# Rows two to a partition, 2 KB runs and one residual tile per unit in a graph-convolution kernel

## The chip, the cores and the metric

The kernel runs on one core of a Trainium2 chip. The metric is the device time of one execution in microseconds (us). The kernel before takes 1714.94 us, the median of the four runs beside which the changed kernel was timed; the prediction was made from three runs with a median of 1718.39 us.

## The reference

```python
# x: (8, 4096, 256), adj: (4096, 4096) sparse, W: (256, 256), all f32
HW = einsum('bnf,fo->bno', x, W)
A_norm = relu((adj + adj.T) * 0.5)
D = sum(A_norm, axis=1);  d = where(D > 0, D ** -0.5, 0)
L = eye(N) - d[:, None] * A_norm * d[None, :]
out = layernorm(x + relu(einsum('nm,bmo->bno', L, HW)))    # over the 256 features
```

## The kernel before

**Part A** symmetrises `adj` tile by tile into DRAM, sums the degrees, and forms g, the rows of HW scaled by d. A *form* makes 128 rows of g for all eight batches. TensorE transposes x, ScalarE copies the transposes from PSUM, TensorE multiplies by W, and ScalarE copies the result out. For every form two symmetrised tiles are made in the first half of part A, and one later on.

```python
def form(m, known):                            # 32 of these
    xin = ...; nc.sync.dma_start(xin, x[:, m*P:(m+1)*P, :]...)     # 1 KB runs
    for b in range(0, B, 2):                   # 4 x 4 = 16 transposes
        pt = psum.tile(...)
        ... nc.tensor.transpose(pt[:, k, c, :], xin[:, b+k, ...], ident)
        nc.scalar.copy(xt[:, b:b+2], pt)
    for b in range(0, B, 2):                   # 4 x 8 matmuls (two passes each)
        ... nc.tensor.matmul(pg..., lhsT=xt[:, b+k, c, :], rhs=w_sb[:, c, :], ...)
        nc.scalar.mul(to, pg, r[:, m:m+1])     # or a copy, scaled later ("held")
    nc.scalar.dma_start(g_dram[m*P:(m+1)*P, :], g)                 # 8 KB runs
```

**Part B** makes the output in sixteen units of 256 rows, each of two blocks of 128. A unit needs only the columns in which its rows have an entry. Lists of these columns are sorted by *pattern* (which of the unit's four groups of 64 rows have an entry) and gathered by indirect DMA into a ring of 13 tiles. `CAPS` gives each unit its number of tiles per pattern. Tiles that are not full cost TensorE as much as full ones. Then for each block:

```python
def finish(i):
    y = evict(i, py.pop(i), ypool)             # ScalarE: PSUM -> SBUF with relu
    def rest():
        z = xr.pop(i)
        mv, rstd = moments(i, y, z, stat)      # VectorE: z += y, statistics
        def end():
            normalise(i, z, mv, rstd)          # VectorE, then store of 1 MB from SyncE
            if i + 3 < NB:
                xr[i+3] = residual(i+3, ypool) # load of 1 MB, issued from ScalarE
        after(6, end)                          # six matmul steps later
    after(1, rest)
...
xr = ypool.tile([P, B, F], F32, tag="xr", bufs=4)       # the residual buffers
...
after(2, lists, u)    # lists of later units: small matmuls into two PSUM banks of
                      # block 0's tag, then some 25 VectorE operations on them
```

VectorE runs in program order, so the list operations of a unit stand behind the residual add of that unit's block 0.

Of the kernel before, what the change touches and what calls it, by code (L numbers as in the profile page):

```python
# [18 lines left out]
KINDS = [1, 2, 3, 0, 6, 9, 5, 10, 12, 4, 8]  # L19

CAPS = [
    [5, 2, 4, 12, 1, 2, 3, 1, 1, 1, 1],
    [4, 3, 2, 6, 1, 1, 1, 1, 1, 3, 3],
    [4, 3, 1, 4, 1, 1, 1, 1, 1, 3, 3],
    [3, 3, 1, 3, 1, 1, 1, 1, 1, 3, 3],
    [4, 3, 1, 3, 1, 1, 1, 1, 0, 3, 3],
    [3, 3, 1, 2, 1, 1, 1, 1, 1, 3, 3],
    [3, 3, 0, 3, 1, 1, 1, 1, 0, 3, 3],
    [3, 3, 0, 2, 1, 1, 1, 1, 1, 3, 3],
    [3, 3, 0, 2, 1, 1, 1, 1, 1, 3, 3],  # L30
    [3, 3, 0, 4, 0, 0, 0, 1, 0, 3, 3],
    [3, 3, 1, 1, 1, 1, 1, 1, 1, 3, 3],
    [3, 3, 0, 4, 0, 0, 0, 0, 0, 3, 3],
    [3, 3, 0, 4, 0, 0, 0, 0, 0, 3, 3],
    [3, 3, 0, 4, 0, 0, 0, 0, 0, 3, 3],
    [3, 3, 1, 3, 0, 0, 0, 0, 0, 3, 3],
    [3, 3, 1, 3, 0, 0, 0, 0, 0, 3, 3],
# [3 lines left out]
def kernel(  # L41
# [6 lines left out]
):  # L48

# [26 lines left out]
    Q = 64  # L76
    QU = 4
    HOLD = 8
# [5 lines left out]
    mid = KINDS.index(0), KINDS.index(12)  # L84
# [12 lines left out]
    e = const.tile([P, NB], F32, name="e")  # L97
    r = const.tile([P, NB], F32, name="r")
# [45 lines left out]
    own = const.tile([P, QU, 2], F32, name="own")  # L144
    nc.vector.memset(own, 0.0)
    for s in range(QU):
        h = slice((s % 2) * Q, (s % 2 + 1) * Q)
        nc.vector.memset(own[h, s, s // 2 : s // 2 + 1], 1.0)
# [14 lines left out]
    def patterns(u):  # L163

        used = ipool.tile([P, QU, NB], F32, tag="used", name=f"used_{u}", bufs=1)
        nc.vector.tensor_scalar(
            used, part[:, :, u * QU : (u + 1) * QU].rearrange("p m s -> p s m"), 0.0, None, ALU.is_gt
        )
        diag = used[:, :, 2 * u : 2 * u + 2]
        nc.vector.tensor_tensor(diag, diag, own, ALU.max)  # L170
        two = ipool.tile([P, 2, NB], F32, tag="two", name=f"two_{u}", bufs=1)
        uv = used.rearrange("p (b h) m -> p b h m", b=2)
        nc.vector.scalar_tensor_tensor(two, uv[:, :, 1], 2.0, uv[:, :, 0], ALU.mult, ALU.add)
        pat = ipool.tile([P, NB], F32, tag="pat", name=f"pat_{u}")
        nc.vector.scalar_tensor_tensor(pat, two[:, 1], 4.0, two[:, 0], ALU.mult, ALU.add)
        kind = ipool.tile([P, NK, NB], BF16, tag="kind", name=f"kind_{u}")
        nc.vector.tensor_tensor(
            kind,
            pat.unsqueeze(1).to_broadcast([P, NK, NB]),
            kinds.unsqueeze(2).to_broadcast([P, NK, NB]),  # L180
            ALU.is_equal,
        )
        plan[u] = pat, kind
# [34 lines left out]
    def place_rest(u, tot, low):  # L218
# [3 lines left out]
        room = CAPS[u][mid[0]] * P  # L222
# [4 lines left out]
            pos, pos, float(first[u][mid[0]] * P + 1), fits, ALU.add, ALU.mult  # L227
# [47 lines left out]
    def index(u, pl):  # L275
# [9 lines left out]
        m0, m1 = first[u][mid[0]], first[u][mid[1]]  # L285
        for ts, n, k in ((slice(0, m0), NB, 2 * u), (slice(m0, m1), NU, u), (slice(m1, t), NB, 2 * u + 1)):
            nc.vector.tensor_scalar(
                ai[:, ts], low[:, ts], float(n), float(N * n + k), ALU.mult, ALU.add
            )
# [3 lines left out]
    with (  # L293
        tc.tile_pool(name="adj", bufs=4) as apool,
        tc.tile_pool(name="hold", bufs=HOLD) as hpool,
# [14 lines left out]
        def symmetrise(i, j, tij, tji):  # L310
            sym = spool.tile([P, A, S], F32, tag="sym", name=f"sym_{i}_{j}")
            for a in range(A):
# [6 lines left out]
            nc.scalar.activation(sym, sym, AF.Relu, scale=0.5)  # L319
            nc.vector.tensor_reduce(  # L320
                part[:, i * A : (i + 1) * A, j * S // Q : (j + 1) * S // Q],
                sym.rearrange("p a (c q) -> p a c q", q=Q),
# [10 lines left out]
        def degrees(i):  # L333
# [6 lines left out]
            nc.gpsimd.tensor_tensor(r[:, ms], e[:, ms], neg_half[:, :A], ALU.pow)  # L340
# [17 lines left out]
        def form(m, known):  # L358

            xin = xpool.tile([P, B, F], F32, tag="xin", name=f"xin_{m}")  # L360
            nc.sync.dma_start(xin, x[:, m * P : (m + 1) * P, :].rearrange("b p f -> p b f"))
            xt = xpool.tile([P, B, FC, P], F32, tag="xt", name=f"xt_{m}", bufs=1)
            for b in range(0, B, 2):
                pt = psum.tile([P, 2, FC, P], F32, tag="ps", name=f"xtr_{m}_{b}")
                for k in range(2):
                    for c in range(FC):
                        nc.tensor.transpose(pt[:, k, c, :], xin[:, b + k, c * P : (c + 1) * P], ident)  # L367
                nc.scalar.copy(xt[:, b : b + 2], pt)  # L368
            if known:
                g = xpool.tile([P, G], F32, tag="g", name=f"gt_{m}")  # L370
            else:
                g = hpool.tile([P, G], F32, tag="held", name=f"held_{m}")
            for b in range(0, B, 2):
                pg = psum.tile([P, 2 * FO], F32, tag="ps", name=f"pg_{m}_{b}")
                for k in range(2):
                    for c in range(FC):
                        nc.tensor.matmul(  # L377
                            pg[:, k * FO : (k + 1) * FO],
                            lhsT=xt[:, b + k, c, :],
                            rhs=w_sb[:, c, :],  # L380
                            start=(c == 0),
                            stop=(c == FC - 1),
                        )
                to = g[:, b * FO : (b + 2) * FO]
                if known:
                    nc.scalar.mul(to, pg, r[:, m : m + 1])  # L386
                else:
                    nc.scalar.copy(to, pg)
            if known:
                nc.scalar.dma_start(g_dram[m * P : (m + 1) * P, :], g)  # L390
            else:
                held[m] = g

        def release(m):
            g = held.pop(m)
            if m % 2:
                nc.vector.tensor_scalar(g, g, r[:, m : m + 1], None, ALU.mult)
            else:
                nc.scalar.mul(g, g, r[:, m : m + 1])
            nc.scalar.dma_start(g_dram[m * P : (m + 1) * P, :], g)  # L400
# [3 lines left out]
        known, early = [], list(range(NB - HOLD, NB))  # L404
        credit = 0.0
        for i in range(NS):
            diag = stat1.tile([P, A, P], F32, tag="diag", name=f"diag_{i}")
            for j in range(i, NS):
# [6 lines left out]
                while credit >= 1.0 and (known or early):  # L415
                    if known:
                        form(known.pop(0), True)
                    else:
                        form(early.pop(0), False)
                    credit -= 1.0  # L420
                credit = min(credit, 1.0)
            degrees(i)
            for m in range(i * A, (i + 1) * A):
                if m in held:
                    release(m)
            lower_diagonal(i, diag)
            known += range(i * A, min((i + 1) * A, NB - HOLD))
# [18 lines left out]
        for m in known:  # L446
            form(m, True)


    def residual(i, ypool):  # L450
        xr = ypool.tile([P, B, F], F32, tag="xr", name=f"xr_{i}", bufs=4)
        nc.scalar.dma_start(xr, x[:, i * P : (i + 1) * P, :].rearrange("b p f -> p b f"))
        return xr
# [25 lines left out]
    def normalise(i, z, mv, rstd):  # L479
# [10 lines left out]
        nc.sync.dma_start(out[:, i * P : (i + 1) * P, :].rearrange("b p f -> p b f"), z)  # L490
# [25 lines left out]
    with (  # L516
# [10 lines left out]
        def gather(n):  # L527
# [5 lines left out]
            both = len(targets(kind)) == 2  # L533
# [28 lines left out]
        xr = {0: residual(0, ypool)}  # L562
# [3 lines left out]
        def finish(i):  # L566
            y = evict(i, py.pop(i), ypool)

            def rest():
                z = xr.pop(i)  # L570
                mv, rstd = moments(i, y, z, stat)

                def end():
                    normalise(i, z, mv, rstd)
                    if i + 3 < NB:
                        xr[i + 3] = residual(i + 3, ypool)
# [25 lines left out]
        after(4, lambda: xr.update({i: residual(i, ypool) for i in (1, 2)}))  # L602
        for q, (u, step) in enumerate(steps):
            new = q == 0 or steps[q - 1][0] != u
            last = q + 1 == len(steps) or steps[q + 1][0] != u
            if new:
                if u + 2 < NU:
                    spread(u + 2)
                if u + 4 < NU:
                    patterns(u + 4)  # L610
                left = {}
# [21 lines left out]
            for c in range(G // S):  # L633
                for (b, rows, at, gt), new_rows in zip(work, fresh):
                    both = any(len(targets(k)) == 2 for k, t in step)
                    off = b * P if both else 0
                    nc.tensor.matmul(  # L637
                        py[2 * u + b][c][rows, :],
                        lhsT=at[:, off + rows.start : off + rows.stop],
# [29 lines left out]
    with tc.If(short > 0):  # L669
        with (  # L670
# [5 lines left out]
            for i in range(NB):  # L676
                lt = full.tile([P, NB, P], F32, tag="l", name=f"l_{i}", bufs=2)
                nc.sync.dma_start(
                    lt, a_dram[:N, i * P : (i + 1) * P].rearrange("(m p) q -> p m q", p=P)
                )  # L680
                py = [psum.tile([P, S], F32, tag="ps", name=f"pz_{i}_{c}") for c in range(G // S)]
                for m in range(NB):
                    gt = full.tile([P, G], F32, tag="g", name=f"gf_{i}_{m}", bufs=4)
                    nc.sync.dma_start(gt, g_dram[m * P : (m + 1) * P, :])
                    for c in range(G // S):
                        nc.tensor.matmul(
                            py[c],
                            lhsT=lt[:, m, :],
# [4 lines left out]
                y = evict(i, py, ypool)  # L693
                z = residual(i, ypool)
                mv, rstd = moments(i, y, z, stat)
                normalise(i, z, mv, rstd)
# [28 lines left out]
```

## Time and profile before

| | before |
|---|---|
| median | 1714.94 us (1702.32 to 1719.27) |
| part A: start to first gathered matmul | 568 us |
| part B: from there to the end | 1154 us |
| busy share of TensorE, VectorE, GpSimd, ScalarE | 88%, 47%, 48%, 21% |

### The profile page before, as it was taken

What the parts mean: (1) busy time and instruction counts of PE and PEld (TensorE: products, weight loads), DVE (VectorE), ACT (ScalarE), POOL (GpSimd) and SP (SyncE); (2) the same over time, 40 slices, a digit from 0 to 9 for tenths busy, and PEclk for the clock granted to TensorE, in tenths of its full rate; (3) what the DMA queues carried; (4) which work ended last, traced back from release to release, by engine and by line L of the source; (5) the groups of instructions that cost most, each with busy time, mean ns of one, the idle gap of its engine ahead of it and who ended that gap; (6) DMA issues with size and microseconds to landing.
All of it is one profiled execution on the core that took longest, in us unless ns stands there. A gap on an engine that the chain in (4) does not pass through costs nothing.

```text
span 1721.7 us, 18447 instructions
## 1 busy us (share of the span) xinstructions
PE 1508.8 (88%) x6504; PEld 799.3 (46%) x6504; DVE 802.5 (47%) x1832; ACT 357.8 (21%) x453; POOL 829.8 (48%) x1111
## 2 busy tenths in 40 slices
PE   6998787888893799999999999989979889898992
PEld 5887666777783244343433333333324333333330
DVE  4777698864553000241442624624633632641335
ACT  3655443555554000100010000000110110110011
POOL 3010000100012663575868777777777777676650
PEclk8999888899897899999999999999989999899996
DMA  9999989999998994688899999899899799799965
GB/s 333 383 377 371 401 331 394 341 405 378 361 363 336 400 397 154 238 336 291 326 405 343 359 378 365 313 402 356 331 398 369 256 404 364 284 342 369 346 260 182
DMA packets 230964, 591.34 MB, mean 343 GB/s; under 512 B 19781, under 2 KB 118389, under 8 KB 191173
## 3 DMA queue, kind: packets, MB, share of 16 engines
q0 software_dynamic: 58480, 321.34, 48.7%
q1 hardware_dynamic: 100352, 134.23, 22.3%
q10 hardware_dynamic: 72032, 134.51, 20.8%
q8 instruction: 54, 0.88, 0.2%
q14 instruction: 46, 0.38, 0.1%
HBM read 494.47 MB, written 136.34 MB: 366 GB/s over the span
## 4 chain that ended last, share of the span: by engine, by line
PE 32%; DMA 25%; issue 23%; DVE 14%; POOL 2%; ACT 2%; another core or an unknown queue 1%; ACTq 0%; DVEq 0%; POOLq 0%; SPq 0%
PE py L637 26%; DMA out_dram<-xr 12%; DMA xr<-in_x_dram 9%; PE pg L377 4%; DVE xr L482 3%; DVE stats L473 2%; DVE xr L468 2%; DVE sym L318 2%; DMA adj<-in_adj_dram 2%; DVE hot L244 1%; DMA xin<-in_x_dram 1%; ACT sym L319 1%; DVE part L320 1%; DMA a_dram<-sym 1%; PE xtr L367 1%
## 5 line engine op out<-in xcount | busy, mean ns | idle before, releaser
L637 PE MATMUL py<-g,ga 128*64 128x512 f32 (+1 forms) x3368 | 1046.8, 604 | 54.3 <-DMA g<-g_dram,gi 36.6
L637 PEld LDWEIGHTS py<-g,ga 128*64 128x64 f32 (+1 forms) x3368 | 395.9, 156 | 692.8 <-issue 661.6
L544 POOL DMA_INDIRECT g<-g_dram,gi x317 | 388.3, 1225 | 236.1 <-PE py L637 132.5
L535 POOL DMA_INDIRECT ga<-a_dram,ai x317 | 336.4, 1061 | 104.0 <-issue 97.3
L468 DVE TENSOR_TENSOR xr<-xr,y 128x2048 f32<-128x2048 f32 x32 | 73.3, 2289 | 634.7 <-ACT y L458 336.6
L458 ACT ACTIVATE y<-py,minus_r 128x512 f32<-128x512 f32 x128 | 80.5, 688 | 1068.2 <-PE py L637 455.0
L377 PE MATMUL pg<-w_sb,xt 128*128 128x256 f32 x1024 | 249.1, 400 | 30.4 <-ACT xt L368 30.0
L318 DVE TENSOR_TENSOR sym<-tr,adj 128x512 f32<-128x512 f32 x256 | 159.7, 682 | 159.2 <-PE tr L315 108.8
L377 PEld LDWEIGHTS pg<-w_sb,xt 128*128 128x128 f32 x1024 | 200.1, 200 | 71.8 <-ACT xt L368 42.9
L340 POOL TENSOR_TENSOR r<-e,neg_half 128x4 f32<-128x4 f32 x8 | 8.3, 1042 | 445.0 <-DVE e L339 389.8
L315 PE MATMUL tr<-ident,adj 128*128 128x128 f32 x1024 | 132.1, 288 | 46.2 <-DMA adj<-in_adj_dram 25.0
L319 ACT ACTIVATE sym<-sym 128x2048 f32<-128x2048 f32 x64 | 122.3, 1912 | 138.0 <-DVE sym L318 111.2
L315 PEld LDWEIGHTS tr<-ident,adj 128*128 128x128 f32 x1024 | 122.3, 149 | 56.0 <-issue 25.1
L320 DVE TENSOR_REDUCE part<-sym 128x32 f32<-128x2048 f32 x64 | 144.5, 2277 | 6.1 <-ACT sym L319 5.9
L482 DVE TENSOR_SCALAR xr<-xr,mv,rstd 128x256 f32<-128x256 f32 x256 | 87.0, 411 | 48.3 <-POOL rstd L480 48.3
L473 DVE BATCH_NORM_STATS2 stats<-xr 128x6 f32<-128x256 f32 x256 | 87.2, 411 | 0.7
L386 ACT ACTIVATE gt<-pg,r 128x512 f32<-128x512 f32 x96 | 66.1, 690 | 79.8 <-PE pg L377 79.8
L480 POOL TENSOR_TENSOR rstd<-rstd,neg_half 128x8 f32<-128x8 f32 x32 | 54.9, 1715 | 44.0 <-DVE rstd L476 43.4
L367 PE MATMUL xtr<-ident,xin 128*128 128x128 f32 x512 | 69.6, 290 | 5.0 <-DVE sym L318 4.8
L368 ACT COPY xt<-xtr 128x512 f32<-128x512 f32 x128 | 68.8, 582 | 14.6 <-PE xtr L367 10.7
L244 DVE TENSOR_TENSOR hot<-iota_q,at 128x4096 bf16<-128x4096 f32 x16 | 70.6, 4416 | 0.0
L367 PEld LDWEIGHTS xtr<-ident,xin 128*128 128x128 f32 x512 | 62.2, 150 | 9.1 <-DVE sym L318 8.3
(93 smaller groups left out, 378.4 us busy)
## 6 DMA issues: line engine op xcount, KB each, us to landing
adj<-in_adj_dram SPq DMA_DIRECT2D x64, 1024.0 KB
a_dram<-sym ACTq DMA_DIRECT2D x64, 1024.0 KB
xin<-in_x_dram SPq DMA_DIRECT2D x32, 1024.0 KB
xr<-in_x_dram ACTq DMA_DIRECT2D x32, 1024.0 KB
out_dram<-xr SPq DMA_DIRECT2D x32, 1024.0 KB
g_dram<-gt ACTq DMA_DIRECT2D x24, 1024.0 KB
g_dram<-held ACTq DMA_DIRECT2D x8, 1024.0 KB
ga<-a_dram,ai POOLq DMA_INDIRECT x317
```

What stands on the lines that cost most here:

```text
L315: nc.tensor.transpose(pt[:, c * P : (c + 1) * P], tji[:, c, a * P : (a + 1) * P], ident)
L318: nc.vector.tensor_add(sym[:, a, :], pt, tij[:, a, :])
L319: nc.scalar.activation(sym, sym, AF.Relu, scale=0.5)
L320: nc.vector.tensor_reduce(part[:, i * A : (i + 1) * A, j * S // Q : (j + 1) * S // Q], sym.rearrange("p a (c q) -> p a c q", q=Q), AX.X, A ...
L367: nc.tensor.transpose(pt[:, k, c, :], xin[:, b + k, c * P : (c + 1) * P], ident)
L377: nc.tensor.matmul(pg[:, k * FO : (k + 1) * FO], lhsT=xt[:, b + k, c, :], rhs=w_sb[:, c, :], start=(c == 0), stop=(c == FC - 1),)
L468: nc.vector.tensor_add(z, z, y)
L473: nc.vector.bn_stats(stats[:, b, :], z[:, b, :])
L482: nc.vector.tensor_scalar(z[:, b, :], z[:, b, :], mv[:, b, 0:1], rstd[:, b : b + 1], ALU.subtract, ALU.mult,)
L535: nc.gpsimd.indirect_dma_start(out=at if both else at[:, :P], out_offset=None, in_=a_pairs if both else a_rows, in_offset=bass.IndirectOff ...
L544: nc.gpsimd.indirect_dma_start(out=gt, out_offset=None, in_=g_dram, in_offset=bass.IndirectOffsetOnAxis(ap=gi[:, t : t + 1], axis=0), boun ...
L637: nc.tensor.matmul(py[2 * u + b][c][rows, :], lhsT=at[:, off + rows.start : off + rows.stop], rhs=gt[:, c * S : (c + 1) * S], start=new_ro ...
```

## The change

The intent is fewer and longer packets. A unit's 256 rows are laid two on each partition, so x, residual and result move in runs of 2 KB. A unit's two blocks become its even and its odd rows. One residual tile of 2 MB serves a unit, with two such buffers in place of four of 1 MB. The patterns are now of even and odd rows, so `KINDS` and `CAPS` change. In unit 0 the dense tiles go from 12 to 15. Forms are cut by rows and batches: one loads 256 rows of four batches and makes its even and odd half one after the other.

```diff
@@ form
-        def form(m, known):
-            nc.sync.dma_start(xin, x[:, m * P : (m + 1) * P, :].rearrange("b p f -> p b f"))
-            for b in range(0, B, 2):        # 16 transposes, four copies
-            for b in range(0, B, 2):        # 32 matmuls
-                nc.scalar.dma_start(g_dram[m * P : (m + 1) * P, :], g)
+        def form(u, b0, known):
+            nc.sync.dma_start(xin..., x[b0 : b0 + BH, u*2*P : (u+1)*2*P, :].rearrange("b (p k) f -> p b (k f)", k=2))
+            for k in range(2):
+                for b in range(0, BH, 2):   # 8 transposes, two copies
+                for b in range(0, BH, 2):   # 16 matmuls
+                put(u, b0, k, g)            # 512 KB, 4 KB runs
@@ degrees
-            nc.gpsimd.tensor_tensor(r[:, ms], e[:, ms], neg_half[:, :A], ALU.pow)
+            # four small matmuls by `perm` bring the degrees to the new order, then
+            nc.gpsimd.tensor_tensor(r[:, ms], own_e..., neg_half[:, :A], ALU.pow)
@@ part B
-        xr = ypool.tile([P, B, F], F32, tag="xr", name=f"xr_{i}", bufs=4)
-        nc.scalar.dma_start(xr, x[:, i * P : (i + 1) * P, :].rearrange("b p f -> p b f"))
+        z = ypool.tile([P, B, 2, F], F32, tag="z", name=f"z_{u}", bufs=2)
+        nc.scalar.dma_start(z.rearrange("p b k f -> p b (k f)"), rows_of(x, u))
@@
-                    normalise(i, z, mv, rstd)       # stores its block
-                    if i + 3 < NB:
-                        xr[i + 3] = residual(i + 3, ypool)
+                    normalise(i, z, mv, rstd)
+                    if b == 1:
+                        store(u, zs.pop(u))
@@ at the start of unit u
+                if u + 1 < NU:
+                    after(3, lambda v=u + 1: zs.update({v: residual(v, ypool)}))
@@ matmul
-                        lhsT=at[:, off + rows.start : off + rows.stop],
+                        lhsT=at[:, 2 * lo + b : 2 * (lo + rows.stop - rows.start) : 2],
```

(Comments stand for the lines that are left out; `CAPS`, `KINDS` and a fallback path are not shown.)

## The prediction

> **What bounds the kernel now.** I read the page's slices first, then a table of stretches, the chain that ended last, the timeline around one wait, and the DMA packets. The kernel has two parts: to 568 us it makes the symmetric matrix and the scaled features g (part A); then it multiplies sixteen units of 256 output rows with gathered tiles (part B). Columns of the stretches: start and end, length, busy time of PE, PEld, DVE, ACT, POOL, granted clock, DMA share, GB/s.
>
> ```profile
> 0.00:540.00 540.00, 443.35 (x2638) 387.09 (x2638) 367.29 (x536) 273.60 (x324) 48.14 (x441) 0.92 0.99 367
> ...
> 568.00:640.00 72.00, 71.82 (x170) 29.13 (x171) 0.00 (x0) 0.00 (x0) 47.91 (x50) 0.98 1.02 407
> 640.00:745.00 105.00, 105.00 (x349) 40.82 (x348) 24.43 (x72) 5.50 (x8) 49.73 (x42) 1.00 0.59 205
> 745.00:900.00 155.00, 153.47 (x562) 59.68 (x562) 49.70 (x153) 10.37 (x16) 104.07 (x92) 1.00 0.93 349
> ...
> 1100.00:1300.00 200.00, 185.35 (x756) 70.01 (x754) 99.96 (x284) 14.54 (x24) 153.30 (x127) 0.96 0.94 358
> 1300.00:1500.00 200.00, 178.40 (x654) 69.30 (x653) 91.58 (x279) 14.97 (x24) 145.01 (x118) 0.93 0.90 336
> ```
>
> Part A is DMA bound outright (0.99). Unit 0 (568 to 727) is TensorE bound: PE never stops while DMA falls to 0.59, because the ring of 13 gathered tiles is full. From about 745 on DMA is the nearest limit (0.90 to 0.96), with PE not far behind. Why DMA isn't at 1.00 there shows in the chain (start, length, what):
>
> ```profile
> 1235.01 18.25 DMA out_dram<-xr
> 1253.36 24.55 DMA xr<-in_x_dram
> 1277.99 2.31 DVE xr L468
> ...
> 1290.27 4.33 DVE hot L244
> 1294.61 2.58 DVE xr L482 x8
> ...
> 1307.08 38.56 issue
> ```
>
> One turn per unit: store of the result, load of the residual into the freed buffer, residual add, lists, normalise, store. ScalarE issues the loads and also does the evictions, in order, so a load that waits for a store holds the next eviction:
>
> ```profile
> 1321.66 20.73 ACTq L452 DMA_DIRECT2D xr<-in_x_dram  x2
> 1342.50 2.42 ACT L458 ACTIVATE y<-py,minus_r 128x512 f32<-128x512 f32 x4 [53.85 <-DMA out_dram<-xr]
> ```
>
> Two stores of 1 MB, issued at 1297 and 1307, end at about 1342: some 45 us for 2 MB. PE only lost 3.4 us to it here, but it shows how near the loop is to binding.
>
> The queues, with packets, MB and share of 16 engines:
>
> ```profile
> q0 software_dynamic: 58480, 321.34, 48.7%
> q1 hardware_dynamic: 100352, 134.23, 22.3%
> q10 hardware_dynamic: 72032, 134.51, 20.8%
> ```
>
> From the trace's packet records, medians: 1 KB takes 46 ns, 2 KB 84 ns, 4 KB 159 ns, 8 KB 309 ns, which is about 8 ns plus 37.6 ns per KB. Means under load are 48 to 49 ns for 1 KB, 85 to 91 ns for 2 KB and 319 to 337 ns for 8 KB.
>
> **What the skill says.** The Trainium skill, "DMA: Bandwidth & Descriptors", section "Why small descriptors are slow (HBM only)", states a fixed overhead per packet between the two sides of an engine; the 8 ns above agrees in kind. The same page, section "Queues, rings and completion order", says each engine goes round the queues it has work for, packet by packet. The trace agrees: from 565 to 585 us, with residual loads (1 KB) beside gathers (8 KB), loads moved 1.10 MB and gathers 6.93 MB, 14% against 1/9 for one packet each in turn. So 2 KB packets should get about twice the rate against gathers. "SBUF — State Buffer", section "Door 1: The DMA port swizzle (why `[64,N]` ≈ `[32,N]`)", says a read stride up to four fp32 stays within a 16-byte line and costs nothing. The before trace shows only the costly side: a reduction at a stride of 128 bytes takes 756 ns for 352 elements, against 412 ns for 256 adjacent ones. "TensorEngine Tiling (Array Packing)", section "Key Properties", says tiles of the array work independently. The trace agrees: two 64-column matmuls on different halves start within 0.26 us of each other and repeat every 0.429 us, as often as a single 128-column one.
>
> **The change part by part.**
>
> *DMA, part A.* x goes from 32768 packets of 1 KB (mean 48.2 ns) to 16384 of 2 KB (about 88 ns): 1581 minus 1442 engine-us, over 16 engines -8.7 us. The g stores go from 4096 packets of 8 KB (319 ns) to 8192 of 4 KB (about 165 ns): 1308 to 1352, +2.7 us. At 0.99 DMA this is all on the path: -6 us.
>
> *End of part A.* The degrees are now permuted by four small matmuls, a PSUM copy and then the power on GpSimd. Only the last of eight times is exposed: about +2 us, from DVE operations of 0.15 to 0.2 us and small matmuls of 0.2 to 0.4 us with their hand-overs. The degree reduction over 64 columns now reads at 8 bytes; I count 0 (64 x 2.28 us if it kept its rate).
>
> *DMA, part B.* Residual loads and stores: 65536 packets of 1 KB (48 to 49 ns) to 32768 of 2 KB (about 88 ns): 3180 to 2884 engine-us, -18 us; of it about -16 lie after unit 0, where DMA is near its limit. The gathers hardly move: unfilled places of a list are skipped, and the rows a unit needs are the same.
>
> *TensorE.* A half pattern is now 64 even or odd rows of one 128-column half, so other patterns pair. I counted slots (a 128-column target, or two 64-column targets in different halves, for one tile): 287 before, 294 after, each slot 4 chunks x 2 instructions x 0.429 us = 3.43 us. As a check, unit 0 has 44 slots before, 151 us; the chain shows one piece of 157.56 us there. Unit 0 goes to 49, since its four tiles of pattern 5 have no pattern 10 to pair with and its dense tiles go from 12 to 15: +17 us, and unit 0 is TensorE bound, so it is on the path. The other two slots fall in DMA-bound units: 0. The weights are now read at a stride of 8 bytes; loads of 132 to 137 ns (64 columns) hide under 429 ns, and at twice the length a pair would still barely exceed it. I count 0.
>
> *Residual buffers.* Four of 1 MB become two of 2 MB. The instruction order on each engine shows that for most units the load for unit u+1 stands on ScalarE between the last eviction of u and the first of u+1, waits for the store of u-1, and is used by the very next residual add. The normalisation of u-1's second block stands on VectorE after the second add of u. So there is one serial turn per unit: store, load, add, lists, normalise. By round robin, a contended 2 MB transfer is 64 packets per engine x (309 + 84) ns = 25 us. DVE part, from the same steps at 1278 to 1307: 29 us. Turn: 25 + 25 + 29 = 79 us if both transfers are contended, and about 29 + 2 x 8 = 45 us if neither is. Before, the turn on ScalarE was 29 + 45 = 74 us contended. Later units need about 62 us of DMA, so neither turn can be fully contended: when it lags, the ring fills, gathers stop, and transfers go faster. I expect the loop to follow DMA as it does now. The wait for stores becomes shorter (25 for 45 us), but the load, until now a unit ahead, joins the turn. DMA idle from 745 to 1690 is about 75 us now; I give it a gain of 8 us, with 25 us of doubt either way.
>
> *End.* The last store is 2 MB after both blocks, for 1 MB after the second; 1 MB takes 3 to 4 us there: +3 us.
>
> Sum: -6 + 2 - 16 + 17 - 8 + 3 = -8 us, so 1718 - 8 = 1710 us.
>
> **The rivals.** (1) *The loop binds.* Two buffers with load and store in series hold each unit at 65 to 68 us instead of 62: for ten units +30 to +60 us, 1740 to 1770. For it: the serial order above, and the add waiting for a load in the chain now. Against it: the transfers speed up as soon as gathers stop. (2) *The longer runs pay more.* The transfers take half as many turns, the 75 us of idle DMA shrink by half, and unit 0's loss is partly covered: 1670 to 1685. For it: DMA is the limit in both parts, and ScalarE's wait for stores falls. Against it: PE needs some 53 us of 62 per unit and only lost 3.4 us to the wait shown. (3) *Strides cost.* If the degree reduction ran at the 128-byte rate (1.7 times), VectorE would gain 64 x 1.5 = 97 us in part A, where it has 170 us free; perhaps 10 to 30 us would show. If the strided weight loads doubled, pairs would need 530 for 429 ns, tens of us in all. Against it: an 8-byte stride still uses each 16-byte line twice.
>
> **Range and chances.** Gains and losses are each 15 to 25 us and cancel; the kernel itself spreads 17 us over three runs. I say 1710 us, range 1672 to 1752. Faster by over 2% needs rival 2 nearly whole: 0.20. Slower by over 2% needs rival 1 or 3: 0.14. Within 2%: 0.66.
>
> **What would show it.** Part A: x in 2 KB packets, its end at about 564 instead of 568 us. The degree reduction still at 2.28 us; residual and result in 16 transfers of 2 MB each, some 25 us or less each. Unit 0's TensorE piece at 170 to 175 us with DMA near 0.5 in it. Matmul spacing still 0.429 us. DMA share after unit 0 of 0.93 or more. Wrong would be: a DMA share of 0.85 or less in the late units with the chain going store, load, add (rival 1); a longer degree reduction or spacing (rival 3); a unit time well under 60 us (rival 2).

## More of the kernel before

The prediction shows the stretches, the chain and the queues. Three more views matter for what followed. First, one cycle of part A on TensorE in the timeline (start, length, line, shapes, number; in brackets the idle time ahead of it and what ended it):

```profile
68.75 1.99 PE L377 MATMUL pg<-w_sb,xt 128*128 128x256 f32 x8 [0.19 <-ACT xt L368]
71.16 5.45 PE L377 MATMUL pg<-w_sb,xt 128*128 128x256 f32 x24 [0.41 <-ACT xt L368]
...
79.94 1.91 PE L367 MATMUL xtr<-ident,xin 128*128 128x128 f32 x16
82.03 1.99 PE L377 MATMUL pg<-w_sb,xt 128*128 128x256 f32 x8 [0.19 <-ACT xt L368]
```

The same step comes again after 82.03 - 68.75 = 13.28 us. TensorE idles 0.60 us of it. It has next to no slack here, although the DMA share of the stretch is 0.99.

Second, waits over the whole run (waiting engine, what it does, what it waited for; us in total, times, longest):

```profile
DVE xr L468 <- DMA xr<-in_x_dram: 195.3, 9, 39.0
...
POOL g L544 <- PE py L637: 132.5, 72, 10.0
...
PE py L637 <- DVE pos_k L159: 5.1, 3, 3.3
```

The residual add waits for its load nine times. GpSimd issues the gathers, and its wait for TensorE is the wait for a free ring tile. The last line is TensorE waiting for a list operation to give back PSUM banks, which are of the same four that the next unit's block 0 needs: 5.1 us in all.

Third, a group of instructions whose shape the change keeps and whose stride it alters, the degree reduction (count, then busy us and mean ns of one, then idle before):

```profile
L320 DVE TENSOR_REDUCE part<-sym 128x32 f32<-128x2048 f32 x64 | 144.5, 2277 | 6.1 <-ACT sym L319 5.9
```

## The result, and the profile after

The changed kernel takes 1843.17 us, the median of four runs (1840.59 to 1859.13; two further runs took 1844.35 and 1862.34), against 1714.94 us. The ratio is 1.0794, with a 95% interval of 1.0714 to 1.0873: slower by 8%, outside the predicted range. All ratios here are the mean time of one kernel's runs over that of the other's of the same rounds, so they are not quite the ratio of the quoted medians.

The profiled run has a span of 1857.4 us, against 1721.7 us. Part A takes 617 us instead of 568 (+49), part B 1240 instead of 1154 (+86). The stretches of the changed kernel (columns as in the prediction):

```profile
0.00:540.00 540.00, 429.00 (x2502) 371.13 (x2502) 350.20 (x509) 250.98 (x295) 46.68 (x435) 0.91 0.94 347
540.00:600.00 60.00, 34.96 (x200) 30.32 (x200) 24.10 (x43) 28.45 (x35) 8.39 (x14) 0.84 0.71 269
...
1100.00:1300.00 200.00, 172.60 (x696) 67.59 (x698) 77.84 (x224) 12.54 (x20) 137.09 (x116) 0.92 0.87 333
...
1500.00:1700.00 200.00, 139.96 (x525) 57.03 (x524) 81.93 (x244) 12.10 (x20) 109.66 (x92) 0.85 0.73 270
```

In the first 540 us the DMA share is 0.94, for 0.99 before, and the end of part A runs at 0.71. In part B the share is 0.87 from 1100 to 1300 us, where the kernel before had 0.94, and 0.73 from 1500 to 1700. TensorE did not take over: it is busy for 173 and 140 of 200 us there. So in these stretches nothing is at its limit, and some order of waits sets the pace. Three views name it.

**Part A, TensorE's timeline:**

```profile
76.47 1.99 PE L415 MATMUL pg<-w_sb,xt 128*128 128x256 f32 x8 [1.07 <-ACT xt L406]
78.88 1.99 PE L415 MATMUL pg<-w_sb,xt 128*128 128x256 f32 x8 [0.42 <-ACT xt L406]
80.71 1.04 PE L403 MATMUL xtr<-ident,xin 128*128 128x128 f32 x8
82.03 3.72 PE L415 MATMUL pg<-w_sb,xt 128*128 128x256 f32 x16 [0.29 <-ACT xt L406]
...
91.19 1.13 PE L415 MATMUL pg<-w_sb,xt 128*128 128x256 f32 x4 [1.07 <-ACT xt L406]
```

The cycle now takes 91.19 - 76.47 = 14.72 us, 1.4 us more. TensorE idles 1.07 + 0.42 + 0.29 = 1.78 us in it, against 0.60. ScalarE's timeline shows the reason: at 88.75 a relu of 1.91 us begins, and the copy of the first transposes can only follow at 90.57. Before, 16 transposes (1.91 us) covered that relu. Now a half has only 8 (1.04 us), and TensorE stands idle for the difference.

**Part B, the chain of waits,** around one unit:

```profile
1112.26 22.32 DMA out_dram<-z
1134.68 26.39 DMA z<-in_x_dram
1161.18 2.30 DVE z L518
...
1186.68 2.60 DVE z L532 x8
1189.31 23.29 DMA out_dram<-z
```

Store, load, add, lists and statistics, normalise, next store: 1189.31 - 1112.26 = 77.05 us for one unit. The prediction took about 62 us as the unit's DMA time. This unit is one of the longest: counted from the traces' matmul records, the twelve units from the fourth on take 68.5 us each on average, against 62.3 before. What TensorE and VectorE do at the end of that load, in the timeline:

```profile
1152.24 8.80 PE L692 MATMUL py<-g,ga 128*64 128x512 f32 x36
1168.99 31.47 PE L692 MATMUL py<-g,ga 128*64 128x512 f32 x88 [7.95 <-DVE pos_k L177]
```

```profile
1161.18 2.29 DVE L518 TENSOR_TENSOR z<-z,y 128x2048 f32<-128x2048 f32 x1 [40.95 <-DMA z<-in_x_dram]
...
1168.42 0.52 DVE L177 TENSOR_TENSOR pos_k<-incl_k,lists 128x352 f32<-128x352 f32 x1
```

VectorE has idled 40.95 us for the load. TensorE runs out of work at 1152.24 + 8.80 = 1161.0 and goes on at 1168.99, when the list operation `pos_k` has read the first of the lists' two PSUM banks. That operation stands in VectorE's order behind the add that waited. The lateness of a load thus reaches TensorE through PSUM banks. Over the run, in the list of waits:

```profile
DVE z L518 <- DMA z<-in_x_dram: 438.5, 11, 51.1
...
POOL g L596 <- PE py L692: 252.0, 90, 16.2
...
PE py L692 <- DVE pos_k L177: 92.9, 7, 23.4
```

These answer the three lines of before: 195.3 became 438.5 us, 132.5 became 252.0, and 5.1 became 92.9 in seven waits. In all, TensorE idles 152.9 us ahead of gathered matmuls, for 54.3 before. This path is read from the traces; no run moves the lists to other banks. The Trainium skill, "Trainium Kernel Development and Optimization", section "Best Practices", says that "consistent bubbles can mean SBUF/PSUM ran out". This trace agrees: 92.9 us of bubbles end with a PSUM bank coming free.

The strides did nothing:

```profile
L338 DVE TENSOR_REDUCE part<-sym 128x32 f32<-128x2048 f32 x64 | 144.5, 2279 | 7.0 <-ACT sym L336 6.9
```

A degree reduction takes 2279 ns for 2277. The gathered matmuls, whose weights are now read at a stride, take 594 ns for 594 (128 columns) and 611 for 608 (64 columns) when the table keeps the shapes apart, and their weight loads 196 for 190 and 142 for 139 ns.

The granted clock is no rival either. It is lower where TensorE has gaps (0.85 from 1500 to 1700 us), but consecutive 128-column matmuls still start 429 ns apart there by the trace's records, as they do in the kernel before.

The theory before the experiments had three causes: the order of part A's forms, the lead of the residual load in part B, and unit 0's extra tiles. The rivals were: ScalarE held up by issuing the loads, the size of the transfers, and the cost of the strides, which the last table had already ruled out.

### The profile page after: what moved, and what is told of

It is laid out like the page before. It is cut to its first block, busy times and chain, and to the rows that moved or that the text cites. A ratio compares the mean times of both kernels' runs of the same rounds, so it can differ in the third digit from the quotient of the medians. Undisturbed runs are those within 1.5% of the kernel's fastest.

```text
span 1857.4 us, 18612 instructions
## 1 busy us (share of the span) xinstructions
PE 1554.8 (84%) x6560; PEld 837.8 (45%) x6560; DVE 804.8 (43%) x1843; ACT 360.9 (19%) x457; POOL 812.7 (44%) x1105
## 4 chain that ended last, share of the span: by engine, by line
PE 33%; DMA 24%; issue 21%; DVE 16%; ACT 3%; POOL 2%; ACTq 0%; DVEq 0%; POOLq 0%; SPq 0%
PE py L692 27%; DMA z<-in_x_dram 10%; DMA out_dram<-z 8%; PE pg L415 5%; DVE sym L335 3%; DMA a_dram<-sym 3%; DVE z L532 2%; DVE stats L523 2%; DVE z L518 2%; DMA g<-g_dram,gi 2%; ACT sym L336 1%; DVE part L338 1%; ACT xt L406 1%; DVE hot L261 1%; DMA adj<-in_adj_dram 1%
## 5 line engine op out<-in xcount | busy, mean ns | idle before, releaser
L692 PE MATMUL py<-g,ga 128*64 128x512 f32 (+1 forms) x3360 | 1074.9, 605 | 152.9 <-DVE pos_k L177 92.9
L692 PEld LDWEIGHTS py<-g,ga 128*64 128x64 f32 (+1 forms) x3360 | 421.2, 161 | 794.0 <-issue 655.4
L596 POOL DMA_INDIRECT g<-g_dram,gi x312 | 369.6, 1185 | 354.6 <-PE py L692 252.0
L518 DVE TENSOR_TENSOR z<-z,y 128x2048 f32<-128x2048 f32 x32 | 73.3, 2291 | 738.4 <-DMA z<-in_x_dram 438.5
L415 PE MATMUL pg<-w_sb,xt 128*128 128x256 f32 x1024 | 262.1, 409 | 54.4 <-ACT xt L406 50.0
L370 POOL TENSOR_TENSOR r<-own_e,neg_half 128x4 f32<-128x4 f32 x8 | 8.4, 1052 | 490.3 <-DVE minus_e L378 359.6
L338 DVE TENSOR_REDUCE part<-sym 128x32 f32<-128x2048 f32 x64 | 144.5, 2279 | 7.0 <-ACT sym L336 6.9
L532 DVE TENSOR_SCALAR z<-z,mv,rstd 128x256 f32<-128x256 f32 x256 | 87.0, 412 | 52.2 <-POOL rstd L530 43.2
L523 DVE BATCH_NORM_STATS2 stats<-z 128x6 f32<-128x256 f32 x256 | 87.0, 411 | 0.7
```

Source lines behind the costliest of these rows:

```text
L338: nc.vector.tensor_reduce(part[:, i * A : (i + 1) * A, j * S // Q : (j + 1) * S // Q].rearrange("p a (h b) -> p a h b", b=2), sym.rearrang ...
L415: nc.tensor.matmul(pg[:, d * FO : (d + 1) * FO], lhsT=xt[:, b + d, c, :], rhs=w_sb[:, c, :], start=(c == 0), stop=(c == FC - 1),)
L518: nc.vector.tensor_add(z, z, y)
L523: nc.vector.bn_stats(stats[:, b, :], z[:, b, :])
L532: nc.vector.tensor_scalar(z[:, b, :], z[:, b, :], mv[:, b, 0:1], rstd[:, b : b + 1], ALU.subtract, ALU.mult,)
L596: nc.gpsimd.indirect_dma_start(out=gt, out_offset=None, in_=g_dram, in_offset=bass.IndirectOffsetOnAxis(ap=gi[:, t : t + 1], axis=0), boun ...
```

## The experiments

Twelve kernels ran in three sessions, all with correct results. The kernel before had a median of 1711.80 us in the first (seven runs), 1704.96 in the second (seven) and 1710.63 in the third (eleven).

### Part B: a third buffer

`b3_three` gives the residual three buffers. They need 16 KB more on each partition, so the ring falls to 11. `b4_ring11` takes only the smaller ring and is its control.

```diff
-    RING = 13
+    RING = 11                  # both
-        z = ypool.tile(..., tag="z", bufs=2)
+        z = ypool.tile(..., tag="z", bufs=3)      # b3_three only
```

> The changed kernel with three residual buffers of 2 MB instead of two, and for the space a ring of 11 gathered tiles instead of 13. To be read against b4_ring11, which has the ring of 11 alone. T1 or T2: a load waits for a store of a unit earlier, its data is there before the add, so part B falls by 50 to 80 us against b4_ring11, and the waits of the residual add for the load (438 us in the trace of the changed kernel) fall under 150 us. Rival T3 (TensorE's 294 slots for 287, or 2 KB packets that slow the gathers): within 15 us of b4_ring11.

> The changed kernel with a ring of 11 gathered tiles instead of 13 and nothing else: the control for b3_three. All theories: 0 to 25 us slower than the changed kernel, 1843 to 1870 us, since gathers run less far ahead.

Measured: `b3_three` 1768.26 us, ratio 1.0326 (1.0271 to 1.0382); `b4_ring11` 1827.08 us, ratio 1.0664 (1.0613 to 1.0716). The third buffer is worth 1827 - 1768 = 59 us, and part B's span goes from 1210 to 1152 us, about the 1154 us of before. The add's wait for its load, 351.4 us in `b4_ring11`, is gone from the list. One wait and one stretch of `b3_three`:

```profile
PE py L692 <- DVE pos_k L177: 6.4, 3, 3.7
```

```profile
1500.00:1700.00 200.00, 193.71 (x691) 79.00 (x691) 85.72 (x263) 20.04 (x32) 148.78 (x125) 1.00 0.97 367
```

TensorE's wait for the banks is gone (6.4 us), and it is busy for 194 of 200 us where it had 140. In `b4_ring11` the same wait is 51.8 us. That a ring of 11 is some 1.3% faster than one of 13 was not expected. Its wait is also shorter than the 92.9 us of the changed kernel. But the two were timed in different sessions and their intervals just touch (1.0716 and 1.0714), so the gain is barely clear of noise, and why a smaller ring should help stays open.

### Part B: one buffer fewer in the kernel before

`e1_three` is the kernel before with three 1 MB buffers in place of four: no 2 MB transfers, no 2 KB packets, no new patterns.

```diff
-        xr = ypool.tile([P, B, F], F32, tag="xr", name=f"xr_{i}", bufs=4)
+        xr = ypool.tile([P, B, F], F32, tag="xr", name=f"xr_{i}", bufs=3)
```

> The kernel before with three residual buffers of 1 MB instead of four, all else as it was: does a load that is no longer ahead cost there as well, with 1 KB runs and blocks of natural rows? T1: yes, the load for a block then waits for a store of the block just before, 30 to 90 us slower, 1740 to 1800 us. If the loss of the changed kernel came from the transfers of 2 MB or the 2 KB packets as such, this stays within 10 us of before.

Measured: 1847.21 us, ratio 1.0809 (1.0778 to 1.0841). One buffer taken from the kernel before costs as much as the whole change, and far more than the 30 to 90 us expected; why so much, no run says. Its waits:

```profile
DVE xr L468 <- DMA xr<-in_x_dram: 477.2, 20, 39.6
...
PE py L637 <- DVE pos_k L159: 33.4, 5, 17.4
```

These were 195.3 and 5.1 us: the same waits grow as in the changed kernel. So a shorter lead of the load is enough to cause them, without larger transfers or packets; and `b3_three` loses them with transfers of 2 MB and packets of 2 KB in place. With four buffers a load fills the one whose store was issued a block earlier; with three it waits for the store just issued, as it does with two of 2 MB.

### Part B: the store earlier, and the load from another engine

`b1_early` normalises one step after the statistics instead of six, so the store leaves sooner. `b2_sp` issues the loads from SyncE, so that a load that waits for a buffer holds no eviction on ScalarE.

```diff
-                after(6, end)
+                after(1, end)                       # b1_early
-        nc.scalar.dma_start(z..., rows_of(x, u))
+        nc.sync.dma_start(z..., rows_of(x, u))      # b2_sp
```

> The changed kernel with two buffers and a ring of 13, only the normalisation asked for one step after the moments instead of six. T1 in its detail (the store of u-1 begins late because its second normalisation stands behind both residual adds of u): the store comes some 10 to 15 us earlier in each of some twelve units, while the load still ends in the turn: 20 to 60 us come back, 1785 to 1823 us. Rival (only the number of buffers matters, or the ring): under 10 us.

> The changed kernel, with the residual loads issued from SyncE instead of ScalarE, so that a load that waits for a store no longer holds the evictions. Theory T1 (the serial turn store, load, add, normalise through two 2 MB buffers costs the 80 us of part B): the turn is the same, at most 20 us come back, 1820 to 1845 us. Theory T2 (ScalarE held by the load is what costs): 60 to 80 us come back, 1765 to 1785 us.

Measured: `b1_early` 1783.16 us, ratio 1.0432 (1.0403 to 1.0460), which is 60 us less than the changed kernel with the same two buffers, at the upper end of what was expected. TensorE's wait for `pos_k` falls from 92.9 to 27.3 us. `b2_sp` 1846.56 us, ratio 1.0780 (1.0725 to 1.0835): no gain. Its waits say why:

```profile
DVE z L518 <- DMA z<-in_x_dram: 355.3, 9, 50.4
...
PE py L692 <- DVE pos_k L177: 83.2, 6, 21.7
```

ScalarE's waits for a store, 153.0 us in the changed kernel, are gone from the list, but the load still comes late and the banks are still held for 83.2 us. The rival of ScalarE's queue falls. What counts is when the store before the load is issued.

### Part A: the form in one piece

`a1_form` does the transposes and copies of both halves ahead of both halves' matmuls, the order of before. `a2_put` adds to it one store of 1 MB per form in place of two of 512 KB; for room, four small degree tiles have one buffer each.

```diff
+            xts = []
             for k in range(2):
                 ... transposes and copies ...
+                xts.append(xt)
+            for k, xt in enumerate(xts):
                 ... matmuls and evictions ...
-                put(u, b0, k, g)               # a2_put: twice 512 KB
+            put(u, b0, g2)                     # a2_put: once 1 MB
```

> The changed kernel, with the transposes and copies of both row halves of a form ahead of all its matmuls, as before the change; the DMA is untouched. Theory A: part A grew by 49 us (first gather matmul at 617 us for 568) because each form now goes twice round between TensorE and ScalarE, and TensorE's turn per form is 14.8 us for 13.3. Then the first gather matmul comes back to 565 to 575 us and the time falls by some 45 us, to about 1798 us. Rival: the 4 KB stores of g or the 2 KB loads of x slow part A; then nothing moves, 1835 to 1850 us.

> a1_form, and besides one store of 1 MB per form for g, as before the change, in place of two of 512 KB (still in runs of 4 KB); four small tiles of the degrees are single buffered for the space. In a1_form part B began at 587 us, 19 us later than before the change. Theory A2: the 32 extra stores cost it, since fewer bytes are in flight and ScalarE's issues wait: part B then begins at 568 to 576 us, some 1800 to 1807 us in all. Rival: the permuted degrees or the 4 KB runs cost it; then it stays at 583 to 588 us and 1812 to 1822 us.

Measured: `a1_form` 1817.34 us, ratio 1.0607 (1.0548 to 1.0667), 26 us less than the changed kernel by the medians. TensorE's timeline has the old cycle back:

```profile
86.78 1.99 PE L418 MATMUL pg<-w_sb,xt 128*128 128x256 f32 x8 [0.19 <-ACT xt L407]
...
97.97 1.91 PE L404 MATMUL xtr<-ident,xin 128*128 128x128 f32 x16
100.07 1.99 PE L418 MATMUL pg<-w_sb,xt 128*128 128x256 f32 x8 [0.19 <-ACT xt L407]
```

The cycle is 100.07 - 86.78 = 13.29 us, as before, and part A ends at 587 instead of 617 us. At 1.4 us a form these 30 us are some 21 of the 32 forms. In other stretches TensorE waits for `adj` (4.6 us ahead of the transposes at 303 us in the changed kernel), so not every form counts. The expectation, 565 to 575 us and some 45 us back, was met by two thirds. `a2_put` ends part A at 578 us, but its ratio of 1.0626 (1.0570 to 1.0681) can't be told from that of `a1_form`: the 1800 to 1807 us that were expected did not come. Some 10 us of part A are still missing there; `d1_natural` below comes back to them.

### Unit 0: four empty slots in the kernel before

`p1_pad` gives unit 0 of the kernel before two more dense tiles. They stay empty and cost TensorE two targets each, four slots in all.

```diff
-    [5, 2, 4, 12, 1, 2, 3, 1, 1, 1, 1],
+    [5, 2, 4, 14, 1, 2, 3, 1, 1, 1, 1],
```

> The kernel before the change, with two more (empty) dense tiles in unit 0, so 4 more TensorE slots of 3.43 us there and two gathers that move almost nothing: a measure of what TensorE time in unit 0 is worth, as the change adds 5 slots there. Theory T3 (unit 0 is TensorE bound): +12 to +16 us, 1724 to 1728 us. Rival: DMA catches it up later, within 5 us of before, about 1712 us.

Measured: 1727.88 us, ratio 1.0131 (1.0079 to 1.0182): +22 us, with 13 to 31 in the interval. In the chain, TensorE's first piece of unit 0:

```profile
564.73 171.31 PE py L637 x448
```

It was 157.56 us for 416 matmuls, as the prediction shows; 32 more take 13.75 us, which is the predicted 3.43 us a slot. All of it reaches the end of the kernel, and perhaps a little more. In the changed kernel unit 0 has 432 matmuls; by the trace's records they last from 616.7 to 791.7 us, 175.0 us and 17.4 more than before.

### The repairs together

`c1_all` puts the repaired form and its single store together with three buffers and a ring of 11. `c2_early` adds the early normalisation.

```diff
  a2_put
-    RING = 13
+    RING = 11
-        z = ypool.tile(..., tag="z", bufs=2)
+        z = ypool.tile(..., tag="z", bufs=3)
-                after(6, end)
+                after(1, end)              # c2_early only
```

> The changed kernel with all three repairs: the order of the form, one store per form, three residual buffers with a ring of 11. If the costs are separate they add: 1768 (b3_three) less 26 (a1_form) less 10 to 15 (a2_put), 1727 to 1733 us, so still a little above before by the extra slots of unit 0. If the repairs share a cause it stays above 1745 us.

> c1_all, and the normalisation asked for one step after the moments instead of six, so stores begin earlier. If the turn through the residual buffers still costs in c1_all: 10 to 30 us less than c1_all. If three buffers have taken it off the path: within 8 us of c1_all, or slower by up to 15 us, since GpSimd then waits for the variances between gathers.

Measured: `c1_all` 1734.85 us, ratio 1.0148 (1.0098 to 1.0199); `c2_early` 1723.88 us, ratio 1.0088 (1.0027 to 1.0148). The differences of ratios along the way add up: 1.0794, less 0.013 for the ring, 0.034 for the buffer, 0.018 for the form (from `b3_three` to `c1_all`, with its single store) and 0.006 for the store, is 1.0088 again, by construction, with each step from one pair of runs. The independent check is that `a1_form` alone gave 0.019 for the form, on another base. The last step, the store, is not clear of noise: the two intervals overlap. The remaining 0.0088 is some 15 us. Two losses are known to be left, unit 0's five extra slots (5 x 3.43 = 17 us) and some 10 us of part A. Together they are more than 15 us, so the later units must have won some back. No run says by what: the early normalisation was not tried on the kernel before.

### The packets alone

`d1_natural` puts part A back to the form of before (1 KB runs of x, 8 KB stores of g, scaled by degrees that are not permuted) and leaves the rest of `c2_early`, the permuted degrees for part B too. `d2_short` is the same with residual and result in runs of 1 KB, each transfer as two of 1 MB. Between the two only the packets of part B and the number of its transfers differ.

```diff
-        nc.scalar.dma_start(z..., rows_of(x, u))
+        for k in range(2):
+            nc.scalar.dma_start(z[:, :, k, :], rows_of(x, u)[:, :, k * F : (k + 1) * F])
-        nc.sync.dma_start(rows_of(out, u), z...)
+        for k in range(2):
+            nc.sync.dma_start(rows_of(out, u)[:, :, k * F : (k + 1) * F], z[:, :, k, :])
```

> c2_early with the form of before: features in blocks of 128 natural rows, x in runs of 1 KB there, g in one store of 8 KB runs, scaled by degrees that are not permuted; only residual and result keep the 2 KB runs and the even and odd rows. In c2_early part B began at 579 us for 568 before. If the divided form is what is left of part A's loss, part B begins at 566 to 572 us and the time falls by 8 to 12 us against c2_early's ratio of 1.0088, to 0.999 to 1.005 of before. Rival: the permutation of the degrees, which stays (off the path of g), or the lists cost it: ratio 1.006 to 1.011.

> d1_natural with each residual load and each store divided in two of 1 MB in runs of 1 KB, the same rows, tiles and order: what the 2 KB runs themselves are worth. DMA is near its limit after unit 0, so by the packet times (2 x 48 ns for 88 ns, 32768 pairs, 16 engines) 16 to 18 us slower than d1_natural. Rival: in this kernel TensorE bounds part B (over 0.95 busy), then under 6 us slower.

Measured, five rounds: `d1_natural` 1729.49 us, ratio 1.0118 (1.0095 to 1.0142); `d2_short` 1732.09 us, ratio 1.0123 (1.0100 to 1.0147). The mean busy time of the DMA engines in part B, summed from the packet records, is 1013 us with 2 KB and 1030 us with 1 KB. So the saving of DMA work is real, 17 us where the prediction had 18, and the time differs by 0.05%, about 1 us, with some 4 us of doubt in either direction. The same stretch, first of `d1_natural`, then of `d2_short`:

```profile
1200.00:1400.00 200.00, 192.12 (x718) 75.67 (x715) 100.07 (x299) 15.62 (x24) 149.02 (x123) 0.98 0.96 361
```

```profile
1200.00:1400.00 200.00, 190.31 (x705) 72.81 (x702) 96.92 (x279) 15.65 (x25) 146.41 (x118) 0.97 0.93 350
```

TensorE is busy for 192 and 190 of 200 us, a share of 0.96 and 0.95, beside a DMA share of 0.96 and 0.93. From 800 to 1600 us TensorE's share is 0.96 in both kernels, and that of DMA 0.93 and 0.94. So with the residual early enough the two stand close together, TensorE slightly ahead, and a saving of DMA work alone brings almost nothing. That TensorE sets the pace is read from these shares; no run tests it.

`d1_natural` missed its own expectation: part B begins at 575 us, and the ratio did not fall to between 0.999 and 1.005. `e1_three`, which has the part A of before and ran in the same session, begins part B at 565 us. So the last 10 us or so do not come from the form. They do not arise at the end of part A either: from the last degree reduction to the first gathered matmul it is 30.7 us in `d1_natural` and 30.5 in `e1_three`. The traces show the loss much earlier. VectorE waits for `perm`, the matrix of the permuting matmuls, which GpSimd makes behind the rest of its set-up:

```profile
16.22 0.75 DVE L166 TENSOR_REDUCE own<-perm 128x2 f32<-128x256 f32 x2 [14.04 <-POOL perm L153]
```

The first degree reduction then ends at 25.1 us, against 21.0 in `e1_three`, and the sixteenth, just after the first degrees, at 137.7 against 130.0. No run moves this set-up, so it is a likely cause of part of the 10 us and not a shown one.

No version beat the kernel before.

## Why the prediction was wrong

**Part A: wrong sign, and the step that failed is "Part A is DMA bound outright (0.99)".** Predicted were -6 us of DMA and +2 us for the degrees; measured were +49 us. A share of 0.99 was read as proof that nothing else mattered. In the stretch that the timeline shows, the TensorE and ScalarE cycle of 13.28 us had next to no slack either, and the change lengthened it to 14.72 us. The prediction never looked at the order inside a form. `a1_form` shows this for 30 of the 49 us in the trace, `a2_put` puts part B some 9 us earlier still, and the last 10 or so are only located. The +2 us for the degrees was about right: from the last degree reduction to the first gathered matmul it is 31.9 us, for 30.5. The -6 us of DMA was not. By the packet records of the changed kernel the 8192 stores of 4 KB took 178.5 ns each and not 165, so they cost 9.6 us more than the 8 KB ones (the prediction had 2.7), which takes away the 8.7 us that it credited to x.

**Part B, residual buffers: right mechanism, and the step that failed is "neither turn can be fully contended", with "I expect the loop to follow DMA as it does now".** The prediction described the serial turn of store, load, add and normalise, put it at 25 + 25 + 29 = 79 us if both transfers are contended, and then set this aside and gave the turn a gain of 8 us. The turn shown measures 77.05 us, 22.32 + 26.39 of them transfers: nearly the contended sum. Over the later units the mean is 68.5 us. Measured by `b3_three` against `b4_ring11`, the lack of a third buffer costs 59 us; by `b1_early`, an earlier store wins 60 us back. So its first rival, "the loop binds", was the truth, at the upper end of its +30 to +60 us, and the argument against it, that transfers speed up as soon as gathers stop, did not save the turn. What the prediction did not see is how a late load reaches TensorE. It is not through ScalarE's queue (`b2_sp`: no gain) but, as the traces show it, through VectorE's order and the list banks in PSUM.

**Part B, the 2 KB runs: the DMA time was right where it was isolated, what it is worth was wrong.** Of -16 us about 1 us arrived in the repaired kernel. In the changed kernel itself it was not isolated; from the kernel before to it, the DMA work of part B hardly moved (1020 and 1022 us by the packet records). The term counted DMA work as path time because DMA was at 0.90 to 0.96, with TensorE "not far behind". In `d1_natural` and `d2_short` TensorE is at 0.96 and DMA at 0.93 and 0.94 once the waits are gone.

**Unit 0: right, in cause and size.** +17 us and a piece of 170 to 175 us were predicted; the trace shows +17.4 and 175.0 us, and `p1_pad` the same cost per slot. The DMA share there was 0.71 (616 to 790 us) and not near 0.5.

**Strides: right.** They were counted as 0; rival 3 falls. (Its factor of 1.7 does not follow from the two times it cites: 756 ns for 352 elements against 412 for 256 is 1.33 times per element.)

**The second rival, that longer runs pay more,** falls with `d2_short`, as far as the repaired kernel goes.

**The range** rested on gains and losses cancelling. The two causes that it lacked or set aside both lie in the order of waits, and both cost time: at least 30 of the 49 us in part A, and some 60 us in part B.

Still open: what causes the last 10 us of part A, why the ring of 11 is faster than that of 13, and why one buffer fewer costs the kernel before 8%.

## What to carry to other kernels

When a change merges small buffers into large ones, count how far ahead of its use each load can start, not the bytes: two buffers of 2 MB gave less lead than four of 1 MB, and taking one of the four away cost 8%. Before crediting a DMA saving, look in the timeline whether another engine's cycle has slack in the same stretch, for two limits can stand side by side: here a DMA share of 0.99 and 0.60 us of slack in a cycle of 13.28. Where an in-order engine waits for a load, ask what stands behind it in its order and which PSUM banks that work holds.

## What the Trainium skill lacked or had wrong

- "Trainium Kernel Development and Optimization", section "Best Practices", advises to double-buffer so that DMA overlaps with compute. Here two buffers of 2 MB were not enough: where a buffer must be stored before it is loaded again, a third one gained 59 us (1827 against 1768 us at the same ring), and an earlier store 60 us (1843 against 1783 us).
- "Perfetto Trace Analysis", section "Identifying the Most-Contended Engine", calls occupancy misleading for the 16 DMA engines and goes by HBM bandwidth instead. In part A both the share (0.99) and the rate (367 GB/s) were high. What the section lacks is the case of two limits at once: TensorE was busy for only 443 of 540 us, yet 1.4 us more in the TensorE and ScalarE cycle lengthened part A by some 30 of its 49 us.
- "DMA: Bandwidth & Descriptors", section "Why small descriptors are slow (HBM only)", is right that each packet carries a fixed cost: 1030 against 1013 us of DMA work in part B. It does not treat what this is worth in time, which was about 1 us here.
- No page describes a late load that holds PSUM banks through an engine's program order: 92.9 us of TensorE's waits, 6.4 us with a third buffer.
